# A planned four-layer graph kernel: ScalarE's prices in the planner, an elu written as one maximum, and the last group's buffer and order

## The chip, the cores and the metric

The kernel runs on one core of a Trainium2 chip. The time is device microseconds of one execution, and its median over the runs is what counts. PE is TensorE (PEld its weight loads), DVE is VectorE, ACT is ScalarE, POOL is GpSimd; SP issues most of the DMAs.

## What is computed

64 graphs of 256 nodes with 128 features go through four layers with one common adjacency matrix, all in fp32. Each layer normalises, applies relu and adds its result to its input:

```python
h = maximum(layernorm(x), 0); x = x + gnn0(h, adj)   # attention over all pairs of nodes
h = maximum(layernorm(x), 0); x = x + gnn1(h, adj)   # gated sums, elu
h = maximum(layernorm(x), 0); x = x + gnn2(h, adj)   # tanh attention
h = maximum(layernorm(x), 0); x = x + gnn3(h, adj)   # a gated recurrent step, five times
```

Layer 0 is the heavy one: for each pair (i, j) of nodes it forms `h = leaky(s1[i] + s2[j] + b)` over 256 channels and `e[i, j] = sum(h * a)`. Layer 1 matters for one edit:

```python
recv = elu(concat(agg, self_part) @ Wn + bn)
out  = concat(recv, x_h) @ Wm + bm
```

## The kernel before

**Work.** The graphs form 34 groups: two of one graph, thirty of two, two of one (`GROUPS`). A group's tiles in the later layers are 512 columns wide, those of a group of one graph 256.

**Layer 0 (class Pairs).** A graph takes 32 rows. A row has one or two batches of 16 tiles of 128 x 256, one tile for each node and half of the neighbours. A tile is relu(s2 + s1[i]) or, with another offset, max(s2, -s1[i]), and any of three engines can make it: ACT one tile an instruction (L669), POOL one tile (L674), DVE four tiles (L657). A full batch `r` (11 buffers) is multiplied on PE into `e_ps` by four matmuls (L722; each shows as two records in the trace). A row with two batches can be *merged*: DVE then adds the second half onto the first with eight scalar_tensor_tensor (L691), and PE multiplies once in place of twice.

**Order.** No scheduler on the chip or in the compiler chooses the order: `tc.manual_schedule()` keeps the order in which the program records its instructions. The recording loop at the end of the kernel has a clock for each of PE, DVE, ACT and POOL (`model.t`), adds a price in ns for each instruction recorded (`act(...)`, `dve(...)`, `pool(...)`, `mm(...)`, `Model.TILE`, `HALF`, `MERGE`, `BATCH`), and each time records what can start first by these clocks. So a price sets nothing on the chip itself, but it decides which engine makes which tile, how many rows are merged, and what stands behind what in each engine's queue. An ACT instruction costs

```python
model.op("act", 40 + n * 0.833 + 42 * sbuf + (0, 103, 196)[pointers] + 49 * table + more)
```

and a tile by ACT 357, by POOL 453.

**Chains.** All that isn't a batch is a step of a chain, a queue of generators that yield the engine of their next step: `ahead` (layer 0's heads and senders), `behind` (layer 0's softmax), `chain12` (layers 1 and 2), `chain3` (layer 3), and for the last two groups `chain4` (the last but one) and `chain5` (the last). Chains are paced while batches are made; at the end, from the last two graphs on, they are not. Layer 3 of the last two groups starts when no batch is left (`last_rest`), in buffers that nothing else needs by then: PSUM banks of layer 0, and for its SBUF tiles `rp`'s `r` buffers (class Home).

**Layer 1 (L793 to L799).** `elu(p, bias)` is three engines' steps: DVE `mn = min(p + bias, 0)`; ACT `p = relu(p + bias)` in PSUM and `mn = exp(mn)`; DVE `(mn - 1) + p`. It is called twice a group, the second time for `rc_t`.

**Layer 2 (L934, L936).** `x3 = o / sum + x2` is written into one of two `x3` buffers, and the step may be recorded only when the group before the group before has been recorded to its end (`counts["out"] >= g - 1`). Layer 3 adds x3 at its very end (`y`, L1041), so the last group's x3 takes the buffer of the third last group and stands behind that group's y.

Of the kernel before, what the change touches and what calls it, by code (L numbers as in the profile page):

```python
# [8 lines left out]
F32 = mybir.dt.float32  # L9
# [3 lines left out]
P = 128  # L13
N = 256
# [23 lines left out]
class Model:  # L38

    TILE = {"act": 357, "pool": 453}
    HALF = 1131
    MERGE = 392
    BATCH = 858
# [9 lines left out]
def kernel(ctx: ExitStack, tc: tile.TileContext, ins: dict, out: bass.AP):  # L55
# [32 lines left out]
    def dve(n, pointers=0, more=0):  # L88
        model.op("dve", 66 + n * 1.042 + 60 * pointers + more)
        return nc.vector  # L90

    def act(n, pointers=0, sbuf=0, table=0, more=0):
        model.op("act", 40 + n * 0.833 + 42 * sbuf + (0, 103, 196)[pointers] + 49 * table + more)
        return nc.scalar

    def pool(ns):
# [35 lines left out]
    def constant(shape, name):  # L132
        return const.tile(shape, F32, name=name)
# [224 lines left out]
    mask_h = constant([P, 2, N], "mask_h")  # L358
    wt_rep = constant([P, P], "wt_rep")
    be_h = constant([P, 1], "be_h")  # L360
    qk = constant([P, P], "qk")
    w34_t = constant([P, P], "w34_t")
    ws = {k: constant([P, P], "t_" + k) for k in ("w3_w", "w4_w", "w5_w")}
# [4 lines left out]
    def constants1():  # L368

        yield "dve"  # L370

        dve(2 * N).tensor_scalar(mask_h, adj_t, 0.0, 0.5 * 0.005, ALU.is_equal, ALU.mult)
        yield "dve"
        dve(2 * N).scalar_tensor_tensor(mask_h, adj_t, 0.5, mask_h, ALU.mult, ALU.add)
        yield "dve"

        dve(P).tensor_scalar(bm_bc, bm_bc, 0.5, None, ALU.add)

        dve(P).memset(wt_rep, 1.0)
        dve(P).tensor_scalar(wt_rep, wt_rep, we[:, 1:2], None, ALU.mult)  # L380
        yield "dve"
        dve(1).tensor_copy(wn1[:, P : P + 1], we[:, 0:1])
        dve(1).tensor_scalar(be_h, be_bc, 0.5, None, ALU.mult)

        def transposed(t, src, scale=1.0):
            yield "pe"
            tp = psum_a([P, P], "w_ps")
            tr(tp, src)
            yield "dve"
            dve(P).tensor_scalar(t, tp, scale, None, ALU.mult)  # L390


        q_t, k_t = raw["L2_gnn_q"], raw["L2_gnn_k"]
        yield from transposed(q_t, q_t)
        yield from transposed(k_t, k_t)
        yield "pe"
        qk_ps = psum_a([P, P], "qk_ps")
        mm(qk_ps, lhsT=q_t, rhs=k_t, start=True, stop=True)
        yield "dve"
        dve(P).tensor_copy(qk, qk_ps)  # L400

        for k, t in ws.items():
            yield "dve"
            r = raw["L3_gnn_" + k]
            dve(P).tensor_tensor(r[:, 0:P], r[:, 0:P], r[:, P : 2 * P], ALU.add)
            yield from transposed(t, r[:, 0:P])
        yield from transposed(u3_t, raw["L3_gnn_u3_w"])
        yield from transposed(u5_th, raw["L3_gnn_u5_w"], 0.5)
        yield "dve"

        dve(P).tensor_tensor(w34_t, ws["w3_w"], ws["w4_w"], ALU.subtract)
        yield "dve"
        for t, a, b, scale in (
            (bz, "w3_b", "u3_b", 0.5), (br, "w4_b", "u3_b", 0.5), (bh, "w5_b", "u5_b", 1.0),
        ):
            dve(1).tensor_tensor(t, biases[a], biases[b], ALU.add)
            if scale != 1.0:
                dve(1).tensor_scalar(t, t, scale, None, ALU.mult)
# [51 lines left out]
    def first_head(xt, to, snd):  # L470

        G, _, W = sizes(xt)
        h = yield from ln_relu(ap, xt, "h0", "h0", at=LANDS)
        h_t = yield from transpose_blocks(ap, h, "h0t", psum_h)
        to.update(h=h, h_t=h_t)
        yield "pe", lambda: counts["w_p"] > 1
        s2_ps, s1_ps = psum_h([P, 2, N], "s2_ps"), psum_a([P, 2, W], "s1_ps")
        for half, p in ((1, s2_ps), (0, s1_ps)):
            for ec in range(2):
                mm(  # L480
                    p[:, ec, :], lhsT=w_p[:, half, bass.ts(ec, P)], rhs=flat(h_t),
                    start=True, stop=True,
                )
        yield "dve"
        s1n = ap.tile([P, 2, W], F32, tag="s1n", name="s1n")
        for ec in range(2):
            dve(W, 1).tensor_scalar(
                s1n[:, ec, :], s1_ps[:, ec, :], -1.0, blin_n[:, ec : ec + 1], ALU.mult, ALU.add
            )
        yield "act"  # L490
        s2 = ap.tile([P, 2, N], F32, tag="s2", name="s2")
        act(2 * N).copy(s2, s2_ps)
        s1 = ap.tile([P, 2, W], F32, tag="s1", name="s1")
        for ec in range(2):
            act(W, 1).activation(
                s1[:, ec, :], s1_ps[:, ec, :], AF.Identity, bias=blin_p[:, ec : ec + 1]
            )
        to.update(s1=s1, s1n=s1n)
        snd.update(s2=s2, s2_ps=s2_ps)

    def head(xt, to):
        G, _, W = sizes(xt)
        h = yield from ln_relu(ap, xt, "h0", "h0")
        h_t = yield from transpose_blocks(ap, h, "h0t", psum_h, settled)
        to.update(h=h, h_t=h_t)
        if counts["left"] > 0:
            yield from bounds(to)
        for ec in range(2):
            yield "pe", lambda: counts["w_p"] > 0
            p = psum_h([P, W], "s1_ps")  # L510
            mm(
                p, lhsT=w_p[:, 0, bass.ts(ec, P)], rhs=flat(h_t), start=True, stop=True
            )
            yield "act", lambda: counts["w_p"] > 1
            if ec == 0:
                s1 = ap.tile([P, 2, W], F32, tag="s1", name="s1")
                s1n = ap.tile([P, 2, W], F32, tag="s1n", name="s1n")
            act(W, 1).activation(s1[:, ec, :], p, AF.Identity, bias=blin_p[:, ec : ec + 1])
            yield "act"
            act(W, 1).activation(  # L520
                s1n[:, ec, :], p, AF.Identity, bias=blin_n[:, ec : ec + 1], scale=-1.0
            )
        to.update(s1=s1, s1n=s1n)
# [54 lines left out]
    class Pairs:  # L578
# [40 lines left out]
        def own(self, who):  # L619

            if who == "dve":
                return self.snd["s2_ps"]
            if who == "act":

                self.by_act += 1
                if self.by_act == 2:
                    t = self.owned[who] = ps_c.tile([P, 2, N], F32, tag="s2_act", name="s2_act")
                    act(2 * N, sbuf=1).copy(t, self.snd["s2"])
                if self.by_act <= 2:
                    return self.snd["s2"]  # L630
            return self.owned[who]
# [96 lines left out]
    def softmax0(g, b, of, e_ps, snd):  # L728
# [12 lines left out]
        for ic in range(2):  # L741
            yield "act"
            if ic == 0:
                pm = ap.tile([P, 2, N], F32, tag="pm", name="pm", bufs=1)
                rs = sp.tile([P, 2], F32, tag="rs", name="rs")
            act(N, 1, more=114).activation(  # L746
                pm[:, ic, :], e_ps[:, ic, :], AF.Exp, bias=nmax[:, ic : ic + 1], scale=-1.0,
                accum_out=rs[:, ic : ic + 1],
            )
# [10 lines left out]
                )  # L760
        yield "act"
        pt = ap.tile([P, 2, N], F32, tag="pt", name="pt", bufs=1)
        act(2 * N).activation(pt, pt_ps, AF.Copy, scale=0.5)
        yield "pe"
        o_ps = e_ps[:, :, 0:P]
        for ic in range(2):
# [5 lines left out]
        for ic in range(2):  # L772
            yield "act"


            act(P, 2).activation(o_ps[:, ic, :], o_ps[:, ic, :], AF.Tanh, scale=rh[:, ic : ic + 1])  # L776
        yield "dve", lambda: counts["x1"] >= g - 2
        if b == 0:
            x1s[g] = ap.tile([P, 2 * GROUPS[g], P], F32, tag="x1", name="x1", bufs=3)
# [8 lines left out]
    def elu(p, bias, tag, home):  # L788
# [8 lines left out]
        yield "dve"  # L797
        o = bp.tile([P, W], F32, tag=home, name=tag)
        dve(W).scalar_tensor_tensor(o, mn, -1.0, p, ALU.add, ALU.add)  # L799
        return o  # L800

    def layer1(x1):
# [65 lines left out]
                    start=(b == 0 and jc == 0), stop=False, skip_group_check=True,  # L868
                )
        mm(rc_ps, lhsT=wn2, rhs=self_t, start=False, stop=True, skip_group_check=True)  # L870
        rc_t = yield from elu(rc_ps, bn, "rc_t", "h")
        yield "pe"
        o1_ps = psum_a([P, G, P], "o1_ps")
        for g in range(G):
# [11 lines left out]
    def layer2(x2, when):  # L886
# [34 lines left out]
        for b in range(NB):  # L921
# [6 lines left out]
                        start=(mc == 0), stop=(mc == 1),  # L928
                    )
            yield "dve", when  # L930
            if b == 0:
                x3 = bp.tile([P, G, P], F32, tag="x3", name="x3", bufs=2)
            rv = sp.tile([P, 2], F32, tag="rv", name="rv")
            dve(2, more=120).reciprocal(rv, o_ps[:, :, P])  # L934
            for c in range(2):
# [108 lines left out]
    def first_rest(g, x1):  # L1044
        x2 = yield from layer1(x1)

        x3 = yield from layer2(x2, lambda: counts["out"] >= g - 1)
        hn = yield from ln_relu(bp, x3, "h3", "h3", lambda: counts["h3"] >= g)
        h_t = yield from transpose_blocks(bp, hn, "h3t", psum_a)
        lane = {len(GROUPS) - 1: chain5, len(GROUPS) - 2: chain4}.get(g, chain3)  # L1050
# [93 lines left out]
    while True:  # L1144
        paced = 0 < n < len(graphs) - 2
        if not making and n < len(graphs) and "s2" in sent[n]:
# [5 lines left out]
            begin(n)  # L1152
            n += 1
        best = None
        for e in ("pe", "dve", "act", "pool"):
            for k, chain in enumerate(chains):
                if chain.engine == e:
                    at = chain.start(paced)
                    if at is not None and (best is None or at < best[0]):
                        best = (at, k, chain.step)  # L1160
            if e == "pe":
# [84 lines left out]
```

## Time and profile before

| | us |
|---|---|
| median of 3 runs | 5093.61 (5093.56 to 5097.92) |
| the profiled execution | 5105.21, of which the span is 5103.4 |
| ACT tiles, L669 (9896 + 512 instructions) | busy 4599.9 + 343.1 |
| POOL tiles, L674 (10136) | busy 4607.8 |
| DVE makes, L657 (1830, four tiles each), and merges, L691 (4904) | busy 2127.0 and 2002.6 |
| PE, L722 (27864 records) | busy 3305.0 |
| granted TensorE clock | 0.998 |

A group's row of the page gives the source line, engine and operation, the tiles written and read, shape and count, then busy time (overlaps counted once) and mean length of one, then the engine's idle time ahead of it and what ended most of that. Lengths of ACT and PE instructions overlap, so a mean length is not what one costs. In the timeline a row is a run of like instructions: start, length from its first start to its last end, and the count. A row of the chain gives start, time and work of each link of the chain that ended last.

### The profile page before, as it was taken

The page shows a single profiled execution, that of the slowest core. Times are in us where ns is not written, and L with a number is a line of the kernel's source. Part 1 is how long each engine was busy: PE and PEld are TensorE (multiplying, and loading weights), DVE is VectorE, ACT ScalarE, POOL GpSimd, SP SyncE. Part 2 cuts the span into 40 slices and gives each one's busy share as a digit, 9 for nine tenths or more (in the row PEclk, how much of TensorE's full clock was granted, in tenths as well). Part 3 has the DMA queues.
Part 4 walks back from the last instruction along what each step waited for, and adds up shares of the span by engine and source line. Part 5 has one row for each costly group of instructions (what it writes and reads, how often), then busy time and mean ns, then how long its engine had stood idle before and what let it go on. Part 6 is the DMA issues. An engine that isn't in the chain of part 4 may idle for free. (4 is left out here: it accounts for less than half of the span.)

```text
span 5103.4 us, 152791 instructions
## 1 busy us (share of the span) xinstructions
PE 5025.8 (98%) x57339; PEld 1999.6 (39%) x57339; DVE 4937.8 (97%) x9638; ACT 5010.9 (98%) x13144; POOL 4855.5 (95%) x10761
## 2 busy tenths in 40 slices
PE   9999999999999999999999999999999999999997
PEld 3434343433333433433333343333434343333333
DVE  9999999999999999999999999999999999999994
ACT  8999999999999999999999999999999999999994
POOL 8999999999999999999999999999999999999991
PEclk9999999999999999999999999999999999999999
DMA  0000000000000000000000000000000000000000
GB/s 23 4 5 2 5 6 6 6 2 6 6 6 6 2 6 6 6 6 2 6 6 6 6 2 6 6 6 6 2 8 6 6 4 3 5 4 4 4 4 8
DMA packets 56024, 28.07 MB, mean 6 GB/s; under 512 B 20336, under 2 KB 55280, under 8 KB 55280
## 3 DMA queue, kind: packets, MB, share of 16 engines
q1 hardware_dynamic: 54736, 18.04, 1.4%
q8 instruction: 449, 7.36, 0.6%
q14 instruction: 295, 2.42, 0.2%
q10 hardware_dynamic: 544, 0.26, 0.0%
HBM read 9.84 MB, written 8.45 MB: 4 GB/s over the span
## 5 line engine op out<-in xcount | busy, mean ns | idle before, releaser
L674 POOL TENSOR_SCALAR r<-s,s1n 128x256 f32<-128x256 f32 x10136 | 4607.8, 522 | 59.0 <-PE e_ps L722 27.2
L669 ACT ACTIVATE r<-s_act,s 128x256 f32<-128x256 f32 x9896 | 4599.9, 1491 | 0.5 <-PE e_ps L722 0.4
L722 PE MATMUL e_ps<-r,a_win 128*32 128x512 f32 x27864 | 3305.0, 593 | 8.3 <-DVE r L691 4.9
L657 DVE TENSOR_TENSOR r<-s_ps,s1n 128x1024 f32<-128x1024 f32 x1830 | 2127.0, 1210 | 0.6 <-PE e_ps L722 0.6
L691 DVE SCALAR_TENSOR_TENSOR r<-s_ps,s1n,r 128x256 f32<-128x256 f32 x4904 | 2002.6, 472 | 1.6 <-ACT r L669 1.3
L722 PEld LDWEIGHTS e_ps<-r,a_win 128*32 128x32 f32 x27864 | 959.9, 110 | 1726.4 <-issue 1271.4
L669 ACT ACTIVATE r<-s,s 128x256 f32<-128x256 f32 x512 | 343.1, 1567 | 0.0
L450 ACT ACTIVATE h<-x,bsh,brs 128x128 f32<-128x128 f32 x384 | 336.2, 1503 | 6.1 <-POOL bsh L444 3.7
L1011 ACT ACTIVATE hv_ps<-hv_ps,bh 128x512 f32<-128x512 f32 (+1 forms) x170 | 267.1, 1571 | 9.4 <-PE hv_ps L108 9.4
L1009 ACT ACTIVATE gate_ps<-gate_ps,bz 128x512 f32<-128x512 f32 (+1 forms) x170 | 271.0, 1594 | 3.1 <-PE gate_ps L108 3.1
L991 ACT ACTIVATE m_ps<-gate_ps,br 128x512 f32<-128x512 f32 (+1 forms) x170 | 258.4, 1520 | 11.3 <-PE gate_ps L108 10.6
L981 ACT COPY m_t<-m_ps 128x512 f32<-128x512 f32 (+1 forms) x170 | 256.1, 1507 | 11.3 <-PE m_ps L108 11.3
L108 PE MATMUL m_ps<-adj_t,hn 128*32 128x256 f32 x4096 | 259.5, 383 | 4.9 <-ACT hn L1032 4.9
L1032 ACT COPY hn<-hn_ps 128x512 f32<-128x512 f32 (+1 forms) x136 | 201.2, 1480 | 19.6 <-PE hn_ps L115 19.6
L108 PEld LDWEIGHTS m_ps<-adj_t,hn 128*32 128x32 f32 x4096 | 140.8, 111 | 129.0 <-issue 38.2
L108 PE MATMUL hv_ps<-rh,u_th 128*32 128x512 f32 (+1 forms) x1360 | 179.0, 568 | 3.5 <-DVE rh L994 3.5
L108 PE MATMUL gate_ps<-m_t,w_t 128*32 128x512 f32 (+1 forms) x1360 | 179.1, 568 | 2.2 <-ACT m_ps L991 2.2
L108 PE MATMUL gate_ps<-m_t,t_w_w 128*32 128x512 f32 (+1 forms) x1360 | 173.8, 574 | 6.2 <-ACT m_t L981 5.4
L108 PE MATMUL hv_ps<-m_t,t_w_w 128*32 128x512 f32 (+1 forms) x1360 | 179.3, 569 | 0.0
L843 ACT ACTIVATE th_ps<-th_ps,a_src 128x256 f32<-128x256 f32 x128 | 178.4, 1394 | 0.8 <-DVE hf L1021 0.8
L746 ACT ACTIVATE pm<-e_ps,nmax 128x256 f32<-128x256 f32 x128 | 174.4, 1364 | 1.8 <-DVE nmax L737 1.7
L776 ACT ACTIVATE e_ps<-e_ps,rh 128x128 f32<-128x128 f32 x128 | 162.7, 1271 | 0.4 <-ACT m_ps L991 0.3
(210 smaller groups left out, 5312.4 us busy)
## 6 DMA issues: line engine op xcount, KB each, us to landing
xt<-in_x_dram SPq DMA_DIRECT2D x30, 256.0 KB
out_dram<-y SPq DMA_DIRECT2D x30, 256.0 KB
row<-rows SPq DMA_DIRECT2D x128, 0.5 KB
xt<-in_x_dram SPq DMA_DIRECT2D x4, 128.0 KB
out_dram<-y SPq DMA_DIRECT2D x4, 128.0 KB
bound<-row SPq DMA_DIRECT2D x30, 2.0 KB
raw_L_gnn_w_w<-in_L_gnn_w_w_dram SPq DMA_DIRECT2D x3, 128.0 KB
adj_n<-in_adj_dram ACTq DMA_DIRECT2D x1, 256.0 KB
```

The lines of the kernel that those rows point to most:

```text
L108: nc.tensor.matmul(out[bass.ts(c, 32), :], lhsT=lhsT[:, bass.ts(c, 32)], rhs=rhs, **flags)
L450: act(P, 2, 1).activation(h[:, g, :], xt[:, g, :], AF.Relu, bias=shift[:, g : g + 1], scale=rstd[:, g : g + 1],)
L657: nc.vector.tensor_tensor(r[:, 2 * g2 : 2 * g2 + 2, :, :], s2[:, ec : ec + 1, :].unsqueeze(1).to_broadcast([P, 2, 2, N]), self.s1n_v[:, ec ...
L669: nc.scalar.activation(r[:, g, ic, :], s2[:, ec, :], AF.Relu, bias=s1[:, ec, i : i + 1])
L674: nc.gpsimd.tensor_scalar(r[:, g, ic, :], s2[:, ec, :], FLT_MAX, s1n[:, ec, i : i + 1], ALU.min, ALU.max,)
L691: nc.vector.scalar_tensor_tensor(r[:, g, ic, :], self.own("dve")[:, 1, :], self.of["s1n"][:, 1, i : i + 1], r[:, g, ic, :], ALU.max, ALU.add,)
L722: nc.tensor.matmul(self.e_ps[bass.ts(g, 32), :, :].rearrange("p a b -> p (a b)"), lhsT=a_win[:, batch["ec"], 31 - t : 63 - t], rhs=flat(r[ ...
L981: act(W).copy(m_t, m_ps)
L991: act(W, 1).activation(t_r, g_ps, AF.Tanh, bias=br, scale=0.5)
L1009: act(W, 1).activation(t_z, g_ps, AF.Tanh, bias=bz, scale=0.5)
L1011: act(W, 1).activation(cand, hv_ps, AF.Tanh, bias=bh)
L1032: act(W).copy(hn, tp)
```

## The change

- *Prices.* ACT's formula and its tile price are replaced: `50 + n * 0.832 + 69 * sbuf + (0, 75, 154)[pointers] + 11 * table`, tile 365; POOL's tile 454. Some calls get a `more` or a `table`: +27 for the four Identity activations with a bias that write SBUF, `table=1` for the copy s2_act and the Copy with a scale.
- *elu_1.* The second elu becomes ACT relu(-p - bn) into SBUF, ACT exp of its negative, and one DVE maximum: `max(p + bn + 1, exp(min(p + bn, 0)))`, which is elu + 1. The 1 is taken back in the constants: the column sums of Wm's first half, by a matmul with ones, are subtracted from bm once.
- *x3.* The last group's x3 goes into an `r` buffer, and its step no longer waits for other groups.
- *Urgent chain.* When no batch is being made any more, the first of `behind`, `chain12`, `chain5` that has a step is urgent: a step of another chain on the same engine that could start now is put behind the urgent step if that one could start within 900 ns.

```diff
-    TILE = {"act": 357, "pool": 453}
+    TILE = {"act": 365, "pool": 454}
...
-        model.op("act", 40 + n * 0.833 + 42 * sbuf + (0, 103, 196)[pointers] + 49 * table + more)
+        model.op("act", 50 + n * 0.832 + 69 * sbuf + (0, 75, 154)[pointers] + 11 * table + more)
...
-        dve(P).tensor_scalar(bm_bc, bm_bc, 0.5, None, ALU.add)
+        dve(1).tensor_scalar(bn_minus, bn, -1.0, None, ALU.mult)
+        dve(1).tensor_scalar(bn_plus, bn, 1.0, None, ALU.add)
+        yield "pe"
+        sum_ps = psum_a([P, P], "sum_ps")
+        mm(sum_ps, lhsT=ones, rhs=wm[:, 0, :], start=True, stop=True)
+        yield "dve"
+
+        dve(P).scalar_tensor_tensor(bm_bc, bm_bc, 0.5, sum_ps, ALU.add, ALU.subtract)
...
+    def elu_1(p, minus, plus, tag, home):
+        W = p.shape[1]
+        yield "act"
+        mn = bp.tile([P, W], F32, tag="elu_m", name="elu_m")
+        act(W, 1, more=27).activation(mn, p, AF.Relu, bias=minus, scale=-1.0)
+        yield "act"
+        act(W, sbuf=1).activation(mn, mn, AF.Exp, scale=-1.0)
+        yield "dve"
+        o = bp.tile([P, W], F32, tag=home, name=tag)
+        dve(W, 1).scalar_tensor_tensor(o, p, plus, mn, ALU.add, ALU.max)
+        return o
...
-        rc_t = yield from elu(rc_ps, bn, "rc_t", "h")
+        rc_t = yield from elu_1(rc_ps, bn_minus, bn_plus, "rc_t", "h")
...
-            if b == 0:
+            if b == 0 and when:
                 x3 = bp.tile([P, G, P], F32, tag="x3", name="x3", bufs=2)
+            elif b == 0:
+                x3 = rp.tile([P, G, P], F32, tag="r", name="x3")
...
-        x3 = yield from layer2(x2, lambda: counts["out"] >= g - 1)
+        x3 = yield from layer2(x2, None if g == len(GROUPS) - 1 else lambda: counts["out"] >= g - 1)
...
+        urgent = None
+        if n == len(graphs) and not making and not doing:
+            urgent = next((c for c in (behind, chain12, chain5) if c.engine), None)
         for e in ("pe", "dve", "act", "pool"):
             for k, chain in enumerate(chains):
                 if chain.engine == e:
                     at = chain.start(paced)
+                    if urgent and at is not None and chain is not urgent and urgent.engine == e:
+                        due = urgent.start(paced)
+                        if due is not None and due < at + 900:
+                            at = max(at, due + 1)
```

More of the change, by code (lines that the diff above doesn't have):

```diff
@@ L360 @@
     be_h = constant([P, 1], "be_h")
+    bn_minus, bn_plus = constant([P, 1], "bn_minus"), constant([P, 1], "bn_plus")
     qk = constant([P, P], "qk")
@@ L494, in first_head @@
         for ec in range(2):
-            act(W, 1).activation(
+            act(W, 1, more=27).activation(
                 s1[:, ec, :], s1_ps[:, ec, :], AF.Identity, bias=blin_p[:, ec : ec + 1]
@@ L517, in head @@
                 s1n = ap.tile([P, 2, W], F32, tag="s1n", name="s1n")
-            act(W, 1).activation(s1[:, ec, :], p, AF.Identity, bias=blin_p[:, ec : ec + 1])
+            act(W, 1, more=27).activation(s1[:, ec, :], p, AF.Identity, bias=blin_p[:, ec : ec + 1])
             yield "act"
-            act(W, 1).activation(
+            act(W, 1, more=27).activation(
                 s1n[:, ec, :], p, AF.Identity, bias=blin_n[:, ec : ec + 1], scale=-1.0
@@ L627, in own @@
                     t = self.owned[who] = ps_c.tile([P, 2, N], F32, tag="s2_act", name="s2_act")
-                    act(2 * N, sbuf=1).copy(t, self.snd["s2"])
+                    act(2 * N, table=1).copy(t, self.snd["s2"])
                 if self.by_act <= 2:
@@ L745, in softmax0 @@
                 rs = sp.tile([P, 2], F32, tag="rs", name="rs")
-            act(N, 1, more=114).activation(
+            act(N, 1, more=119).activation(
                 pm[:, ic, :], e_ps[:, ic, :], AF.Exp, bias=nmax[:, ic : ic + 1], scale=-1.0,
@@ L762, in softmax0 @@
         pt = ap.tile([P, 2, N], F32, tag="pt", name="pt", bufs=1)
-        act(2 * N).activation(pt, pt_ps, AF.Copy, scale=0.5)
+        act(2 * N, table=1).activation(pt, pt_ps, AF.Copy, scale=0.5)
         yield "pe"
@@ L773, in softmax0 @@
             yield "act"
-            act(P, 2).activation(o_ps[:, ic, :], o_ps[:, ic, :], AF.Tanh, scale=rh[:, ic : ic + 1])
+            act(P, 1).activation(o_ps[:, ic, :], o_ps[:, ic, :], AF.Tanh, scale=rh[:, ic : ic + 1])
         yield "dve", lambda: counts["x1"] >= g - 2
```

## The prediction

> **What bounds the kernel now.** I read the page's first part, then the costliest groups, then the busy times by stretch, then timelines of single engines, and last the chain that ended last.
>
> ```profile
> PE 5025.8 (98%) x57339; PEld 1999.6 (39%) x57339; DVE 4937.8 (97%) x9638; ACT 5010.9 (98%) x13144; POOL 4855.5 (95%) x10761
> ...
> L674 POOL TENSOR_SCALAR r<-s,s1n 128x256 f32<-128x256 f32 x10136 | 4607.8, 522 | 59.0 <-PE e_ps L722 27.2
> L669 ACT ACTIVATE r<-s_act,s 128x256 f32<-128x256 f32 x9896 | 4599.9, 1491 | 0.5 <-PE e_ps L722 0.4
> L722 PE MATMUL e_ps<-r,a_win 128*32 128x512 f32 x27864 | 3305.0, 593 | 8.3 <-DVE r L691 4.9
> L657 DVE TENSOR_TENSOR r<-s_ps,s1n 128x1024 f32<-128x1024 f32 x1830 | 2127.0, 1210 | 0.6 <-PE e_ps L722 0.6
> L691 DVE SCALAR_TENSOR_TENSOR r<-s_ps,s1n,r 128x256 f32<-128x256 f32 x4904 | 2002.6, 472 | 1.6 <-ACT r L669 1.3
> ```
> ```profile
> 150.00:4850.00 4700.00, 4659.90 (x53042) 1850.51 (x53038) 4615.35 (x8985) 4692.26 (x12321) 4586.16 (x10150) 1.00 0.02 5
> ```
> The stretch row gives PE, PEld, DVE, ACT and POOL busy in 4700 us. Four engines look full, so the small differences decide: ACT is idle for 7.7 us, PE for 40.1, DVE for 84.7, POOL for 113.8. ACT's L669 waits for nothing (0.5 us in 9896 instructions). But its mean of 1491 ns can't be its price: 9896 times 1491 ns is three times the span. Several ACT instructions are open at once, so the price is the distance between their ends (start plus length) in the timeline.
>
> ```profile
> 2503.61 0.97 ACT L1032 COPY hn<-hn_ps 128x512 f32<-128x512 f32 x1
> 2504.08 4.89 ACT L669 ACTIVATE r<-s_act,s 128x256 f32<-128x256 f32 x12
> ...
> 2514.89 1.16 ACT L466 COPY h_t<-h_t_ps 128x512 f32<-128x512 f32 x1
> 2515.35 6.91 ACT L669 ACTIVATE r<-s_act,s 128x256 f32<-128x256 f32 x17
> ```
> ```profile
> 2503.89 0.37 DVE L434 BATCH_NORM_AGGREGATE bmv<-bst 128x2 f32<-128x6 f32 x4
> 2504.18 0.85 DVE L691 SCALAR_TENSOR_TENSOR r<-s_ps,s1n,r 128x256 f32<-128x256 f32 x2
> 2504.94 11.40 DVE L657 TENSOR_TENSOR r<-s_ps,s1n 128x1024 f32<-128x1024 f32 x10
> ```
> ```profile
> 2506.46 23.63 POOL L674 TENSOR_SCALAR r<-s,s1n 128x256 f32<-128x256 f32 x52
> ```
> From 2504.58 to 2508.97 there are 12 ACT tiles, 366 ns each; from 2516.05 to 2522.26 there are 17, 365 ns each. The planner of before counts 357. In the same way a DVE make (4 tiles) ends 1.131 us after the last (2505.03 to 2516.34, ten of them), a merge 0.39 us (0.77 for two), and a POOL tile takes 454 ns; the planner's 1131, 392 and 453 fit these. So only ACT is priced too low: by some 8 ns in each of 9896 + 512 tiles, 83 us by the end. It has been given more than it can do in the time planned, and the other three wait for it. That is the bound of the first 4990 us.
>
> **A rule weighed against the row.** The page's first line puts PE level with ACT at 98%; by that row PE would be the bound. The Trainium skill's Perfetto Trace Analysis (Identifying the Most-Contended Engine) says that busy time is a fair measure for ScalarE, but for TensorE not, since matmuls are pipelined, and to look at the weight loads' share instead (39% here).
>
> ```profile
> 4988.68 5.15 PE e_ps L722 x48
> ```
> This row of the chain has six batches of eight records in 5.15 us, 0.858 us each. The 27864 records of L722 are 3483 batches, 2988 us at that pace, where their group shows 3305 busy. So some 300 us of PE's busy time is matmuls standing open. I take the rule: PE has room. By the row the sum below would end at no gain (second rival).
>
> **The change part by part.**
>
> The prices (TILE and the act terms) move instructions alone. The instruction order of the changed program has 9772 ACT tiles from s_act for 9896 (-124), 10140 POOL tiles (+4), 1886 DVE makes (+56, that is 224 tiles), 4800 merges (-104), and 13 more PE batches (a tile that isn't merged goes through PE by itself). By engine:
> - ACT: -124 x 0.366 = -45.4 us.
> - DVE: 56 x 1.131 - 104 x 0.39 = +22.8 us.
> - POOL: 4 x 0.454 = +1.8 us.
> - PE: 13 x 0.858 = +11.2 us.
>
> elu_1 takes one instruction from DVE: before, L793 (0.66 between ends at 512 columns, 2519.20 to 2519.86) and L799 (0.60); after, one scalar_tensor_tensor with a pointer, no such row on this tile; the nearest are L793 at 0.66 and L799 at 0.60, and I take 0.66. Saving 0.60 in 30 large groups, 0.34 in four small: -19.4 us of DVE. DVE's whole sum is thus +3.4 us, and its 84.7 us of idle time cover it. ACT keeps two instructions, but its Relu now writes SBUF where L795 wrote back to PSUM. Here a second rule speaks against the change: the Trainium skill's ScalarE: Activation LUTs (What happens when an exp ACTIVATE runs) holds that ACT writes faster to PSUM than to SBUF. The trace agrees, and sizes it:
>
> ```profile
> 310.95 1.28 ACT L669 ACTIVATE r<-s_act,s 128x256 f32<-128x256 f32 x1
> 311.31 1.51 ACT L520 ACTIVATE s1n<-s_ps,blin_n 128x512 f32<-128x512 f32 x1
> ```
> L520 (PSUM to SBUF, with bias) ends 0.59 us after the one before; L795 (PSUM to PSUM, with bias) ends 0.57 after its forerunner (2522.82 to 2523.39). So +0.02 to 0.03 in 34 instructions, +1 us on ACT. The bound is 0 to +2. Without the rule the sum would be 1 us lower, so the edit stands.
>
> The constants (sum_ps: four small matmuls with ones; bn_minus, bn_plus: two DVE columns) come once, in the first 150 us. The matmuls ask for wm's load, issued at the start; behind the DVE instruction that waits for sum_ps stand some merges. I take 0.5 us, from 0 to 2; put into the allowance below. No DMA is added; the last group's store is the last of SP's queue both times.
>
> ACT's sum to its last tile: -45.4 + 1, and +2 since layer 3 of the group before the last two stands further ahead of that point (four to five 512-column ACT instructions at 0.5 us are on the other side): -42.4. Is that gain on the path? ACT is what the others wait for, and each of them has room above its new sum (PE +11.2, DVE +3.4, POOL +1.8). What is late next: DVE, with the least room. ACT also loses part of its backlog, and with it inputs that were always there when it came. I allow +5 us of new ACT waits for that, between 0 (price 365, pace 366: ACT still falls behind the plan a little, so its inputs still come first) and +20 (ACT waiting as much as 25 us or so in the bulk, which would still be a third of what DVE waits there now). Bulk: -37.4, from -45 to -20.
>
> The end. In before, ACT's last tile ends at 4988 and the last e_ps at 5001; 27 merges are left between (27 x 0.39 = 10.5 us of DVE). In the changed order five are left, but 31 e_ps instructions and 16 of layer 3 at a quarter batch each (some 10 us of PE). I take -2, from 0 to -4.
>
> From there the last group runs alone with two layer-3 chains, 102 us. The chain shows one wait that the x3 edit removes:
>
> ```profile
> 5050.50 0.88 PE o_ps L108 x32
> ...
> 5054.93 0.69 DVE y L1041
> 5055.62 0.09 DVE rv L934
> 5055.74 0.61 DVE x L936 x2
> ```
> The last group's o_ps is there at 5051.4, but rv and x3 stand behind y of another group, whose x3 buffer they need: 4.2 us. With x3 in an r buffer (no makes are left to need one) only hf stands ahead: -3.5.
>
> The urgent rule keeps foreign PE blocks from before the last group's. From the two orders, with before's times: ahead of y_ps foreign 3.87 us (5015.45 to 5019.32), now a 512-column gate and hv, 2.58: -1.3. Ahead of rsum m_ps and gate (e_t ends 5025.6, rsum starts 5027.35): now nothing, -1.8. Ahead of rc: -0.8. Ahead of o_ps of layer 1, 3.87 to 2.58, and elu shorter by a DVE step: -1.3. g_ps: -0.7. s_ps, 2.65 to one 0.4 transpose: -2.2. Softmax and first norm (exps without m_t between, tanh without a gate ahead): -3. Sum with x3 -14.6. The price: groups 31 and 32 now run beside layer 3 of the last group, where before four of its five steps ran alone, 6.9 to 8.2 us each. Their PE blocks (0.43 and 0.86) stand in three or four of its steps, part of it under its ACT and DVE work: +3.5, from 0 to +10. Tail: -11, from -18 to -3.
>
> Sum: -37.4 - 2 - 11 = -50.4 us. The profiled execution took 5105.2 (span 5103.4 and 1.8 around it), so it would take 5055. The median of the runs is 5093.6, 11.6 below the profiled one, and no row says that the change touches that gap: 5093.6 - 50.4 = 5043. A measurement of this kernel can tell about 0.2%, 10 us, from no change.
>
> **The rivals.**
>
> 1. *The next engine takes over early.* DVE's 84.7 us of idle time are waits in order (rh for ACT's m_ps 36.2 us in all, rc_t and xh_t for elu_m 31.3), not room that can be filled. If a good part of them stays, the bulk shrinks by 20, not 37: 5093.6 - 20 - 2 - 5 = 5067. For it: the changed plan fills DVE, POOL and ACT together. Against it: many of these waits are for ACT, which is late by the wrong price. Chance 0.15.
>
> 2. *PE was the bound*, as the page's first line has it. Then ACT's 45 us bring nothing, 13 batches cost 11.2, the tail gives 11: 5093, no change. Against it: L722's 0.858 a batch, and weight loads that wait for r of ACT, POOL and DVE over 300 us in all. Chance 0.03.
>
> 3. *ACT's lead time is lost, and it ends slower.* In before ACT runs late against the plan, so nothing it reads is late. Priced right, it comes on time, and each of its 13144 - 10408 - 128 = 2608 instructions that read another engine's fresh result may wait. The place is every m_ps, gate_ps, hv_ps and h. Up to 20 ns a time the 50 us are used up (20 x 2608 = 52 us); above 24 ns it is over 0.2% slower. At 28 ns, 73 us: 5116. For it: the plan's margins are a few hundred ns. Against it: ACT still runs 1 ns a tile over its price and POOL on it, and the others wait for ACT first. Chance 0.04.
>
> That the change doesn't do what it says is excluded for the work moved, since the instruction order shows it; that the tail gains nothing is in the range (5054).
>
> **How the numbers follow.** Likeliest (0.78): 5043; its own range 5030 to 5060 (bulk -45 to -27 and end and tail -22 to -6 give 5027 to 5061 with all at one end). With rival 1 faster has 0.93; rival 2 is no change, 0.03; rival 3 slower, 0.04. The range is 5026 to 5068: below, all three terms at their good ends (-45 - 4 - 18 = -67); above, rival 1.
>
> **What would show it.** Right: ACT tiles still end 365 to 367 ns apart, L676 (the old L669) has 9772 + 512; ACT's last tile ends near 4950, not 4988; DVE's and POOL's idle time in the bulk fall by tens of us; x3 follows o_ps within 1 us; last e_ps to end takes 84 to 99 us. Wrong: ACT idle over 30 us in 150:4850 (rival 3 from 50), PE with no gaps and an unmoved end of the bulk (rival 2), DVE waiting as before with ACT idle too (rival 1), layer-3 steps of the last group of 9 us and more (no gain in the tail).

## The result, and the profile after

The changed kernel takes 5035.28 us (median of 4 runs, 5033.44 to 5042.35), the one before 5093.84: a ratio of 0.9886, 95% interval 0.9872 to 0.9901, or 58.6 us less. The profiled execution took 5042.35, its span 5040.5, against 5105.21 and 5103.4. A second measurement in another set (r_after below) gave 0.9868 (0.9855 to 0.9882).

The first part of the page and the groups of the changed kernel (L676 is the old L669, L681 L674, L729 L722, L664 L657, L698 L691):

```profile
PE 4996.9 (99%) x57451; PEld 1959.9 (39%) x57451; DVE 4933.9 (98%) x9558; ACT 4963.7 (98%) x13020; POOL 4855.9 (96%) x10765
...
L681 POOL TENSOR_SCALAR r<-s,s1n 128x256 f32<-128x256 f32 x10140 | 4608.1, 521 | 42.3 <-PE e_ps L729 11.3
L676 ACT ACTIVATE r<-s_act,s 128x256 f32<-128x256 f32 x9772 | 4465.0, 1201 | 1.6 <-PE e_ps L729 1.6
L729 PE MATMUL e_ps<-r,a_win 128*32 128x512 f32 x27968 | 3282.2, 593 | 3.6 <-DVE r L698 1.7
L664 DVE TENSOR_TENSOR r<-s_ps,s1n 128x1024 f32<-128x1024 f32 x1886 | 2191.4, 1209 | 0.0
L698 DVE SCALAR_TENSOR_TENSOR r<-s_ps,s1n,r 128x256 f32<-128x256 f32 x4800 | 1956.6, 471 | 0.6 <-ACT r L676 0.6
```

Busy time by stretch, changed kernel (PE, PEld, DVE, ACT, POOL):

```profile
150.00:4850.00 4700.00, 4685.82 (x53794) 1829.78 (x53792) 4666.37 (x9036) 4695.01 (x12321) 4627.44 (x10244) 1.00 0.02 5
```

POOL and DVE are hardly busier in all (4855.9 after 4855.5, 4933.9 after 4937.8); they do the same work in a shorter time. In the stretch DVE's idle time falls from 84.7 to 33.6 us, POOL's from 113.8 to 72.6, PE's from 40.1 to 14.2. ACT's falls too, from 7.7 to 5.0: it still waits for next to nothing, with 124 tiles less. Its pace is the old one, by the ends in the timeline:

```profile
2379.77 1.43 ACT L1055 COPY hn<-hn_ps 128x512 f32<-128x512 f32 x1
2380.24 3.16 ACT L676 ACTIVATE r<-s_act,s 128x256 f32<-128x256 f32 x6
2382.66 1.32 ACT L815 ACTIVATE elu_m<-rc_ps,bn_minus 128x512 f32<-128x512 f32 x1
```

Six tiles end between 2381.20 and 2383.40, 367 ns each; elu_1's Relu ends 0.58 us after them (2383.98), against 0.57 for the old Relu into PSUM. The new DVE step:

```profile
2382.64 3.47 DVE L664 TENSOR_TENSOR r<-s_ps,s1n 128x1024 f32<-128x1024 f32 x3
2386.03 0.74 DVE L820 SCALAR_TENSOR_TENSOR rc_t<-rc_ps,bn_plus,elu_m 128x512 f32<-128x512 f32 x1
```

It takes 0.66 us (2386.11 to 2386.77), and no idle time stands before it. DVE's waits for elu_m of rc_t fell from 17.7 us to 4.3; most of that is the prices' doing, since with the old elu and the new prices (e1_prices below) they were 5.3, with the new elu and the old prices (e2_elu) 8.6.

The profiled executions in three parts, from the trace (us from the span's start):

| | before | after | difference |
|---|---|---|---|
| ACT's last tile ends | 4987.7 | 4941.3 | -46.4 |
| from there to the last e_ps | 13.2 | 8.8 | -4.4 |
| from there to the end | 102.5 | 90.4 | -12.1 |

At the end, x3 now follows its o_ps. The timelines of PE and DVE:

```profile
4987.78 1.30 PE L108 MATMUL o_ps<-hv,pm 128*32 128x129 f32 x32 [2.19 <-DVE pm L940]
```
```profile
4989.14 0.17 DVE L957 RECIPROCAL rv<-o_ps 128x2 f32<-128x2 f32 x1 [0.91 <-PE o_ps L108]
4989.34 0.61 DVE L959 SCALAR_TENSOR_TENSOR x<-o_ps,rv,x 128x128 f32<-128x128 f32 x2
...
5011.05 0.68 DVE L1064 TENSOR_TENSOR y<-y_ps,x 128x512 f32<-128x512 f32 x1
```

o_ps ends at 4989.08, rv starts at 4989.14, and the y it would have stood behind comes 22 us later.

### The profile page after: what moved, and what is told of

It reads as the page before. It is cut to its first block, busy times and chain, and to the rows that moved or that the text cites. A ratio compares the mean times of both kernels' runs of the same rounds, so it can differ in the third digit from the quotient of the medians.

```text
span 5040.5 us, 152839 instructions
## 1 busy us (share of the span) xinstructions
PE 4996.9 (99%) x57451; PEld 1959.9 (39%) x57451; DVE 4933.9 (98%) x9558; ACT 4963.7 (98%) x13020; POOL 4855.9 (96%) x10765
## 5 line engine op out<-in xcount | busy, mean ns | idle before, releaser
L681 POOL TENSOR_SCALAR r<-s,s1n 128x256 f32<-128x256 f32 x10140 | 4608.1, 521 | 42.3 <-PE e_ps L729 11.3
L676 ACT ACTIVATE r<-s_act,s 128x256 f32<-128x256 f32 x9772 | 4465.0, 1201 | 1.6 <-PE e_ps L729 1.6
L729 PE MATMUL e_ps<-r,a_win 128*32 128x512 f32 x27968 | 3282.2, 593 | 3.6 <-DVE r L698 1.7
L664 DVE TENSOR_TENSOR r<-s_ps,s1n 128x1024 f32<-128x1024 f32 x1886 | 2191.4, 1209 | 0.0
L698 DVE SCALAR_TENSOR_TENSOR r<-s_ps,s1n,r 128x256 f32<-128x256 f32 x4800 | 1956.6, 471 | 0.6 <-ACT r L676 0.6
L729 PEld LDWEIGHTS e_ps<-r,a_win 128*32 128x32 f32 x27968 | 930.4, 110 | 1720.2 <-issue 1296.1
L676 ACT ACTIVATE r<-s,s 128x256 f32<-128x256 f32 x512 | 324.8, 1407 | 0.0
L457 ACT ACTIVATE h<-x,bsh,brs 128x128 f32<-128x128 f32 x384 | 288.5, 1163 | 0.6 <-POOL bsh L451 0.6
L1032 ACT ACTIVATE gate_ps<-gate_ps,bz 128x512 f32<-128x512 f32 (+1 forms) x170 | 224.2, 1320 | 3.8 <-PE gate_ps L108 3.8
L1004 ACT COPY m_t<-m_ps 128x512 f32<-128x512 f32 (+1 forms) x170 | 217.3, 1278 | 8.7 <-PE m_ps L108 8.5
L1034 ACT ACTIVATE hv_ps<-hv_ps,bh 128x512 f32<-128x512 f32 (+1 forms) x170 | 217.9, 1282 | 8.0 <-PE hv_ps L108 8.0
L1014 ACT ACTIVATE m_ps<-gate_ps,br 128x512 f32<-128x512 f32 (+1 forms) x170 | 215.8, 1270 | 7.0 <-PE gate_ps L108 5.9
L1055 ACT COPY hn<-hn_ps 128x512 f32<-128x512 f32 (+1 forms) x136 | 168.9, 1242 | 13.7 <-PE hn_ps L115 13.7
L108 PE MATMUL gate_ps<-hf,u_t 128*32 128x512 f32 (+1 forms) x1088 | 138.4, 569 | 0.0
```

Source lines behind the costliest of these rows:

```text
L108: nc.tensor.matmul(out[bass.ts(c, 32), :], lhsT=lhsT[:, bass.ts(c, 32)], rhs=rhs, **flags)
L457: act(P, 2, 1).activation(h[:, g, :], xt[:, g, :], AF.Relu, bias=shift[:, g : g + 1], scale=rstd[:, g : g + 1],)
L664: nc.vector.tensor_tensor(r[:, 2 * g2 : 2 * g2 + 2, :, :], s2[:, ec : ec + 1, :].unsqueeze(1).to_broadcast([P, 2, 2, N]), self.s1n_v[:, ec ...
L676: nc.scalar.activation(r[:, g, ic, :], s2[:, ec, :], AF.Relu, bias=s1[:, ec, i : i + 1])
L681: nc.gpsimd.tensor_scalar(r[:, g, ic, :], s2[:, ec, :], FLT_MAX, s1n[:, ec, i : i + 1], ALU.min, ALU.max,)
L698: nc.vector.scalar_tensor_tensor(r[:, g, ic, :], self.own("dve")[:, 1, :], self.of["s1n"][:, 1, i : i + 1], r[:, g, ic, :], ALU.max, ALU.add,)
```

## The experiments

Each was timed beside the kernel before. Chips and even executions differ: the kernel before had medians of 5102.8, 5107.9 and 5094.2 us in the three sets, and the changed program's last ACT tile came at 4941 in one profiled execution and at 4933 in another (r_after). So each kernel is judged by its ratio or against a kernel of its own set, and a part of a trace only where it moves by more than some 5 us, or beside a count that explains it.

The traces show where those 8.7 us come from. Within runs of tiles ACT's ends are 365.1 ns apart on the mean in the first execution and 364.4 in r_after's, POOL's 454.2 and 452.2, while a DVE make (1131.1 and 1131.2) and a PE batch (0.858 us in both) keep their pace; the difference builds up evenly over the whole span. What sets ACT's and POOL's pace in an execution is not shown. That the program followed it agrees with a time that hangs on ACT or POOL, and not on DVE or PE. Before's profile had 365.2 and 454.5, so its comparison with the first profile of the changed kernel is not touched.

### Which part of the change does it

**e1_prices**: the kernel before, with the prices alone.

```diff
-    TILE = {"act": 357, "pool": 453}
+    TILE = {"act": 365, "pool": 454}
...
-        model.op("act", 40 + n * 0.833 + 42 * sbuf + (0, 103, 196)[pointers] + 49 * table + more)
+        model.op("act", 50 + n * 0.832 + 69 * sbuf + (0, 75, 154)[pointers] + 11 * table + more)
```

> The kernel before with the new prices alone (no elu_1, old x3, no urgent chain). Its order has 9780 ACT tiles from s_act (-116), 1905 DVE makes, 4712 merges, 24 more PE batches. Theory (ACT is the bound, everything else waits for it): -116 x 0.366 = -42 us, a little of it lost to waits: 5050 to 5057. Rival (PE is nearly as full): 24 batches x 0.858 = +20 us and no gain, 5090 to 5115. Rival (DVE takes over): some -20, 5074.

Measured: 5051.33, before 5102.82; ratio 0.9897 (0.9882 to 0.9912), so 51.5 us less. That is some eight to nine tenths of what the whole change brings (58.6 us in the first measurement, 66.0 in r_after's set). ACT's last tile ends at 4948.3, 39.4 us earlier than in before's profile, where 116 x 0.366 asked for 42; 24 more PE batches cost nothing that shows. ACT's count is what the time follows. In the stretch ACT is idle for 6.3 us, PE for 13.0:

```profile
150.00:4850.00 4700.00, 4686.99 (x53790) 1830.84 (x53786) 4662.56 (x8971) 4693.73 (x12318) 4627.02 (x10235) 1.00 0.02 5
```

Part of the gain lies at the end, although this kernel has neither tail edit: from the last e_ps to the end it is 96.0 us, where before took 102.5. In the new order the other group's y comes ahead of the last group's o_ps, and rv no longer stands behind it (o_ps ends at 5005.30):

```profile
5001.86 0.69 DVE L1041 TENSOR_TENSOR y<-y_ps,x 128x512 f32<-128x512 f32 x1 [0.68 <-PE y_ps L115]
...
5005.36 0.17 DVE L934 RECIPROCAL rv<-o_ps 128x2 f32<-128x2 f32 x1 [2.07 <-PE o_ps L108]
```

**e2_elu**: the kernel before, with elu_1 (and its constants) alone, as in the change's diff.

> The kernel before with elu_1 alone, at the old prices. DVE is spared 34 instructions, some 19 us; the order gives ACT 20 tiles fewer and PE 9 batches more. Theory: only ACT's count matters, -20 x 0.366 = -7 us, 5087. Rival (DVE's time is the bound's equal): -19 x a third or more, and the chain is one step shorter: 5075 or less. Rival (PE): +8 us, 5102.

Measured: 5087.97, ratio 0.9970 (0.9958 to 0.9981), so 15 us less: between the theory and the DVE rival. ACT's last tile is at 4972.2, 15.5 us earlier. Twenty tiles fewer explain 7 of it, and ACT's idle time from 150 to 4900 us, 7.7 before and 2.6 here, 5 more. The rest is within what two executions differ by (the four profiles with before's order up to the last e_ps have ACT's last tile between 4983.9 and 4987.7). DVE's 19 us weren't turned into time at a third by themselves (its idle time stays, 85.6 to 79.1 us over the same stretch): with the old prices DVE was waiting anyway.

**e3_tail**: the kernel before, with x3 and the urgent chain alone; **x3_only** and **urgent_only** have one of them each.

```diff
-            if b == 0:
+            if b == 0 and when:
                 x3 = bp.tile([P, G, P], F32, tag="x3", name="x3", bufs=2)
+            elif b == 0:
+                x3 = rp.tile([P, G, P], F32, tag="r", name="x3")
...
+        urgent = None
+        if n == len(graphs) and not making and not doing:
+            urgent = next((c for c in (behind, chain12, chain5) if c.engine), None)
```

> The kernel before with the x3 buffer and the urgent chain alone. Tiles, makes and merges are those of before. Theory: the first 5001 us stay, the tail is 10 to 15 us shorter: 5079 to 5084. Rival (interleaving gives back what the order gains): within 4 us of 5094.

Measured: 5091.75, ratio 0.9978 (0.9969 to 0.9986), 11 us less. The last e_ps comes at 4996.3 and the end 93.2 us after it, where before took 102.5: -9.3, short of the 10 to 15 expected.

> The kernel before with the last group's x3 in an r buffer and without its wait for other groups; old prices, old elu, no urgent chain. Tiles and merges are those of before. Theory (each tail edit takes away its own wait): x3 no longer stands behind another group's y, 3 to 4 us shorter after the last e_ps. Rival (the two only work together): within 1.5 us in the tail.

Measured: 5089.1, ratio 0.9992 (0.9983 to 1.0001), which by itself tells nothing; but the end comes 99.1 us after the last e_ps, -3.4 as expected, and x3 starts 0.2 us after its o_ps.

> The kernel before with the urgent chain alone; x3 still waits for the third last group's y. Theory: 5 to 8 us shorter after the last e_ps. Rival (the two only work together): the last group comes to its x3 sooner, but stands there until a y that the rule has put back, and the tail is as long as before or longer by up to 3 us.

Measured: 5096.38, ratio 1.0008 (0.9999 to 1.0017). The end comes 103.8 us after the last e_ps, 1.3 more than before. The theory fell; the rival holds. Timelines of urgent_only, PE and DVE:

```profile
5037.41 1.07 PE L108 MATMUL o_ps<-hv,pm 128*32 128x129 f32 x32
```
```profile
5054.91 0.69 DVE L1041 TENSOR_TENSOR y<-y_ps,x 128x512 f32<-128x512 f32 x1 [0.21 <-PE y_ps L115]
5055.52 0.16 DVE L934 RECIPROCAL rv<-o_ps 128x2 f32<-128x2 f32 x1
```

The last group's o_ps is ready at 5038.5, 13 us sooner than before. Then it stands for 17 us until the other group's y, and rv starts at 5055.52, where before had it at 5055.54. At before's prices the rule needs the buffer: alone -3.4 and +1.3, together -9.3.

For parts as small as these the granted TensorE clock is a rival. After the last e_ps it fell, for stretches of some 3.4 or 6.8 us at a time, to half:

| us | before | x3_only | urgent_only | e3_tail | e1_prices | changed | r_after |
|---|---|---|---|---|---|---|---|
| last e_ps to end | 102.5 | 99.1 | 103.8 | 93.2 | 96.0 | 90.4 | 92.1 |
| granted clock there | 0.945 | 0.961 | 0.960 | 0.976 | 0.897 | 0.958 | 0.939 |
| clock time missing (length x (1 - clock)) | 5.6 | 3.9 | 4.1 | 2.3 | 9.9 | 3.8 | 5.7 |

The last two are the same program: 1.7 us longer with 1.9 us more missing. If all that is missing counts, which is an estimate from this one pair, the tails without it are 96.9, 95.2, 99.7, 90.9, 86.1, 86.6 and 86.4 us. The two edits still work only together at before's prices (-1.7 and +2.8, together -6.0), and the executions of e3_tail at a granted clock of 0.998 over the whole span, 5093.1 to 5093.3 us, stand 9 us under all but one of before's at the same clock in that set, 5102.5 to 5102.9. But e1_prices, without either, comes to as short a tail as the changed kernel: that the tail edits bring anything at the new prices is not shown.

The parts do not add up either: 51.5, 15 and 11 us are 77.5, and the whole brings 58.6 to 66.0.

**e4_tile357**: the changed kernel with one number put back.

```diff
-    TILE = {"act": 365, "pool": 454}
+    TILE = {"act": 357, "pool": 454}
```

> The changed kernel with one number put back: a tile by ACT at 357. Its order has 9944 ACT tiles (172 more than the changed one, 48 more than before). Theory: 172 x 0.366 = +63 us on the changed kernel's 5035, less the waits that ACT has there: 5090 to 5098, no better than before though elu_1 and the tail edits are in. Rival (the price is a small part): 5045 to 5065.

Measured: 5101.65, ratio 0.9996 (0.9988 to 1.0005): no better than before, with elu_1, the tail edits and all other prices in. Its stretch row shows the old picture, ACT idle for 1.6 us, DVE for 100.1 and POOL for 145.2:

```profile
150.00:4850.00 4700.00, 4654.77 (x52896) 1824.67 (x52896) 4599.87 (x8973) 4698.44 (x12342) 4554.84 (x10076) 1.00 0.02 5
```

The 8 ns in a tile's price decide about all that the change is worth.

### Is it ACT, or the wrong price?

**r_after** is the changed kernel again, the measure for the next three.

> The changed kernel once more, beside the next three and on their chip, so that they have a common measure. Both theories: a ratio of 0.987 to 0.990 to before; span parts as in the first profile (ACT's last tile near 4941, last e_ps near 4950, 90 us after it).

Measured: 5041.96, ratio 0.9868 (0.9855 to 0.9882). ACT's last tile 4932.6, last e_ps 4941.4, 92.1 us after it.

**a_tile373** and **a_pool446** each change one number of the changed kernel.

```diff
-    TILE = {"act": 365, "pool": 454}
+    TILE = {"act": 373, "pool": 454}
```
```diff
-    TILE = {"act": 365, "pool": 454}
+    TILE = {"act": 365, "pool": 446}
```

> The changed kernel with a tile by ACT priced too high by as much as it was too low: 373. ACT gets 156 tiles fewer (-57 us), POOL 52 more (+24 us), DVE +23 us. Theory (the engine priced too low is the bound; the fit at 365 is near the best): ACT now has idle time, POOL and DVE are the late ones, and it ends 0 to 12 us slower than the changed kernel. Rival (ACT is costly as such, the less it has the better): 15 us faster or more.

> The changed kernel with POOL priced too low by 8 ns, as ACT was before (446 for 454). POOL gets some 120 tiles more (+54 us at 454), ACT 60 fewer. Theory (it is the wrong price, whichever engine has it, that costs): POOL is the one without idle time, ACT and DVE wait, and it is 15 to 40 us slower than the changed kernel. Rival (only ACT, with its late results in every chain, makes others wait): within 8 us of the changed kernel.

Measured: 5049.51 (ratio 0.9887) and 5080.15 (0.9945), so 7.6 and 38.2 us slower than r_after. Both as the theory had it. (In both profiles ACT's pace is that of the first profile of the changed kernel, 365.1 and 365.2 ns; against that execution they are 7.2 and 38.0 us slower.) Their stretch rows, in this order:

```profile
150.00:4850.00 4700.00, 4688.14 (x53760) 1847.77 (x53758) 4674.51 (x8990) 4654.30 (x12151) 4644.22 (x10274) 1.00 0.02 5
```
```profile
150.00:4850.00 4700.00, 4675.44 (x53234) 1821.43 (x53230) 4617.32 (x8940) 4651.64 (x12169) 4647.93 (x10282) 1.00 0.02 5
```

ACT idles for 45.7 and 48.4 us. With POOL priced too low, POOL is the one that the others wait for: DVE idles for 82.7 us, and ACT's h for POOL's bsh, 2.7 us in all in the changed kernel:

```profile
ACT h L457 <- POOL bsh L451: 43.3, 85, 2.1
```

POOL keeps 52 us of idle time in the stretch, against the expectation of none. Of these, 43 us are some 490 gaps of under 0.15 us, which it has in the other kernels too (40 us before, 43 in the changed one); its longer waits fell from 30.0 us in the changed kernel to 8.6. Pricing ACT 8 ns too high costs a fifth of pricing POOL 8 ns too low. A likely reason, not tested by itself, is that the work then goes to the other engines in small parts, where a price too low heaps it on one.

### How much room PE has

**pe_load** adds matmuls with zero weights, that the planner does not count, ahead of every 32nd batch of the changed kernel.

```diff
+            counts["batch"] = counts.get("batch", 0) + 1
+            loads = [zero_w] * (counts["batch"] % 32 == 0)
...
             for g in range(4):
+                for w in loads:
+                    nc.tensor.matmul(
+                        self.e_ps[bass.ts(g, 32), :, :].rearrange("p a b -> p (a b)"),
+                        lhsT=w, rhs=flat(r[:, g, :, :]), start=False, stop=False,
+                        skip_group_check=True,
+                    )
```

> The changed kernel with PE loaded: every 32nd batch is preceded by four matmuls of the same size with zero weights, which the planner does not price; 436 matmuls, 109 batches, 109 x 0.858 = 94 us of PE. All else in its order is that of the changed kernel. Theory (PE has some 200 us of room, its busy share notwithstanding): 0 to 15 us slower than the changed kernel. Rival (PE at 99% busy is full and next in line): 80 to 94 us slower.

Measured: 5098.79, ratio 0.9985 (0.9976 to 0.9993), 56.8 us slower than r_after (60.6 between the two profiled executions, in which ACT has the same pace). Neither the theory (0 to 15) nor the rival (80 to 94) had it. Of 94 us, 33 to 37 found room and 57 to 61 became time. In its stretch row PE's idle time is 7.3 us and ACT's 48.8:

```profile
150.00:4850.00 4700.00, 4692.69 (x53962) 1885.60 (x53958) 4618.99 (x8916) 4651.17 (x12187) 4557.82 (x10133) 1.00 0.02 5
```

So PE was not the bound of the changed kernel, but by this load it was under 40 us away from being it. The load comes in bursts of 0.86 us that the planner doesn't know of; how much of the loss is such a burst holding up what stands behind it, and how much PE being full, was not separated.

### Is there more to be had

**o_merge393** and **o_367_456** change prices of the changed kernel by a hair.

```diff
-    MERGE = 392
+    MERGE = 393
```
```diff
-    TILE = {"act": 365, "pool": 454}
+    TILE = {"act": 367, "pool": 456}
```

> The changed kernel with a merge priced at 393 for 392: an order that differs throughout (12 ACT tiles more, 24 merges fewer) for a price that is as good. A measure of what the order alone does by chance. Theory: within 8 us of the changed kernel (0.987 of before).

> The changed kernel with the mean distances between ends in place of the median ones: ACT's tile 367, POOL's 456. Theory (the nearer the prices to the pace, the better, but little is left): 0 to 6 us faster than the changed kernel. Rival (the order's chance decides by now): as much as 8 us either way.

Measured: 5037.04 (ratio 0.9887, 0.9872 to 0.9902) and 5035.08 (0.9885, 0.9872 to 0.9899). Both are the changed kernel's 0.9868 to 0.9886 again. Whether the second is better by a few us can't be told; no other kernel here clearly beats the changed one.

## Why the prediction was right

The forecast was 50.4 us less, 58.6 were measured, and for the bulk the mechanism was the one named; for the end only the number was right. Term by term, against the two profiled executions (62.9 us in the spans):

- *ACT is the bound because its tiles are priced too low.* Shown. e1_prices alone gives 51.5 us, e4_tile357 takes everything back with one number, and a_pool446 makes a loss of the same kind, 38 us, out of another engine's price.
- *Bulk: forecast -37.4, profiled -46.4, beyond the -45 it was bounded by.* The mis-sized term is the +5 us of new ACT waits. None came: ACT's idle time in the stretch went from 7.7 to 5.0 us. The rest of the term stands, 124 x 0.366 = 45.4. The reason given for the lower end (the price is 365, the pace 366, so ACT still comes a little late and its inputs are there first) agrees with the kernels in which ACT has its 365 or less and no other engine is priced too low or loaded (1.6 to 7.8 us of idle time). Where ACT is early (a_tile373), or another engine late (a_pool446, pe_load), it waits 46 to 49 us in the stretch. Without the +5 the forecast is -42.4; the other 4 us are about what executions of one order differ by.
- *To the last e_ps: forecast -2, profiled -4.4,* just outside 0 to -4. In the traces 22 merges start after ACT's last tile in before, where the prediction had 27, and none in the changed kernel, where it had five; PE's ten microseconds were 8.8.
- *Tail: forecast -11, profiled -12.1.* From the last e_ps to the last group's x3 it is 39.9 us after 55.4, -15.5 for a forecast of -14.6; from x3 to the end 50.5 after 47.1, +3.4 for +3.5. The list added up well, but that it did is in part luck. Its reading as a sum of separate gains was wrong: of x3's -3.5 and the urgent rule's -11.1 + 3.5, the second exists at before's prices only with the first (urgent_only). And the prices, to which it gave no part of the tail, take 6.5 us out of it by themselves (e1_prices), the wait of x3 among them, or all of it by the estimate that leaves out the clock.
- *elu_1: DVE's 0.60 us a time at no gain, ACT +0.02 to 0.03.* DVE's price was right (0.66). ACT's reading was not: over the 512-column cases the new Relu ends 579 ns (median) after the instruction before it, where the old one took 552, but the exp takes 519 where it took 545, so the pair costs 1098 ns after 1097. The rule that the prediction weighed, in the Trainium skill's ScalarE: Activation LUTs (Step-by-step: what each stage is for), calls PSUM the port of lower latency; the 27 ns agree with that, but they are no price (see the last section). At nothing the edit was too low: e2_elu saves 15 us on the old kernel. What it adds on the new prices was not measured by itself; ACT's last tile comes 7 us earlier in the changed kernel than in e1_prices, at the same pace of ACT.
- *PE has room, by the rule on busy time.* The choice was right, PE was not the bound. The size was wrong: the 300 us read from 0.858 us a batch against 3305 us busy was not room. In pe_load 33 to 37 us were, and the weight loads' share of 39% told nothing of how near the limit was. The batches of a long row follow each other at 0.858 us; what PE pays between unlike matmuls and weights is missing from that row, which is the likely reason and was not tested, and the idle time in the stretch (14.2 us in the changed kernel) was the nearer gauge. The rival "PE was the bound" was given 0.03 on too good a reason; it was some tens of us from true.
- *The rivals.* DVE's waits went with their cause: 84.7 us idle became 33.6, so rival 1 falls. (Of the 36.2 us for m_ps that it counts, only 5.1 lie in the stretch; ACT's elu_m, 29.8 us there, was the wait that mattered.) Rival 3, ACT losing its lead, falls for the price chosen.

The profile and the median stood 11.4 us apart before and 7.1 after, which is the difference between 62.9 and 58.6.

## What to carry to other kernels

In a program whose order is planned by prices, read each engine's price from the distance between ends, and mend first the one that is too low: it makes its engine the bound, and the others wait, often for a third engine. An error of 2% in one price cost 38 us on POOL and 51 to 65 on ACT here (a_pool446; e1_prices and e4_tile357), the same error upward 8. An edit that lets a chain come sooner needs the buffer at the end of that chain to be free, or it only waits at another place.

## What the runs showed of the hardware

The length of an ACT record is no price, but it tells of a backlog. For the same instruction at a pace of 364 to 367 ns, L676's mean length was 1491 ns before and 1201 in the changed kernel, where ACT is the late engine; in a_tile373, where ACT waits for others, it was 689, and in pe_load, where PE is late, 760. (The other two of these kernels agree: 1410 in e4_tile357, 776 in a_pool446.) The groups of those two:

```profile
L676 ACT ACTIVATE r<-s_act,s 128x256 f32<-128x256 f32 x9616 | 3922.9, 689 | 1.4 <-PE e_ps L729 1.4
```
```profile
L678 ACT ACTIVATE r<-s_act,s 128x256 f32<-128x256 f32 x9772 | 4082.4, 760 | 2.6 <-PE e_ps L739 2.4
```

A mean length that grows without the distance between ends growing marked, in these kernels, the engine whose queue was never empty.

ACT's writes to PSUM ended earlier, but the engine was not faster for it. An ACT tile (written to SBUF) ends 392 ns after a forerunner that wrote PSUM (median of 620 in before) and 365 after one that wrote SBUF (of 9001): the 27 ns that the write to PSUM gained stand ahead of the next end. So a price read from one pair of ends needs a forerunner and a follower with the same kind of destination.

PE's busy time had less slack than a count of batches makes it: in pe_load 99% busy was within some 37 us, under 1%, of full.
